# The statements behind the steady loop of a cross-attention kernel, in another order

## The chip, the cores and the metric

The kernel runs on one core of one Trainium2 chip. The metric is the device time of one execution in microseconds (us). The engines are TensorE (PE; its weight loads are PEld), VectorE (DVE), ScalarE (ACT), GpSimd (POOL) and SyncE (SP, which here only issues transfers). Each has its own stream of instructions and waits for the others by semaphores.

## The reference

Cross-attention between a text x (64 batches of 256 x 512) and a context c (64 batches of 256 x 384), all in fp32, with a layer norm on queries, on keys and on the result. For each batch:

```python
text_p  = x @ W_text + b_text            # 256 x 512
audio_p = c @ W_audio + b_audio          # 256 x 512
Q = layer_norm(text_p, g1, beta1)
K = layer_norm(audio_p, g2, beta2)
alpha = softmax(Q @ K.T / sqrt(512))     # 256 x 256
H = (alpha @ audio_p) @ W_out + b_out
out = layer_norm(H + x, g_out, beta_out)
```

## The kernel before

One batch is one step. As the rows of alpha add up to one, alpha @ audio_p @ W_out is taken as (alpha @ c) @ W with one folded weight (`wao_sb`, 384 x 512), and its bias goes in with the start values. The projections and the output product of most batches are done in schemes that save multiplications: the class `Thirds` (L543, keys `k` and the output `o`) multiplies sums of thirds of the operands with sums of thirds of the weights, in steps `one` to `five` (all at L557), between which ScalarE and VectorE put start values into PSUM (`copy_t`, `start_l0`, `start_u`, `take_m`, ...) and evict at the end (`plus_middle`, `plus_ends`, `last_00`, ...). `Fork` (L717) does the same for the queries. `Attention` (L806) holds one batch's scores, softmax, context and output.

The work of a batch is spread over several steps of `for b in range(3, B - 3)`, and `nc` runs under a manual schedule: each engine executes its instructions in the order in which the statements are written. The order is written out, so that a statement of one batch stands between those of three or four others. What hangs together are the data and buffers only: an engine whose next instruction isn't ready waits, and what stands behind it waits with it.

Behind the loop there are some 330 statements that finish the last batches. In them `last_m3` and `old` are batch 60, `settled` and `old_m3` batch 59, `settled_m3` batch 58, `last` and `at_m3` batch 61, `at` batch 62 and `end` batch 63, the last; `q2_m3` and `k2_m3` are batch 63's projections. What the later parts need of them:

- **The round trip of queries and keys.** The normalised rows (`normalise`, ScalarE, L488; in the profile `kr` or `qr`) are stored to memory (`store`, SyncE, L498: `kd<-kr`, `qd<-qr`), fetched back in squares by four transfers (`fetch`, which ends in `squares`, L73: `kq<-kd`, `qq<-qd`) and transposed by VectorE (`turn`, L76). ScalarE then puts gain and bias on (`affine`, L527: `kT`, `qT`), and `score` (L823; by blocks L900) can multiply. SyncE also loads the rows of x and c and stores the results (`out_dram`).
- **The context.** `transpose_e` (TensorE, L978) turns the attention rows `e` into PSUM, `copy_e` (ScalarE, L984) brings them to `eT`, `context_one` and `context_two` (TensorE, L1095) multiply by c, and `copy_one` (L1111) and `copy_two` (L1114) bring the result `zT` out of `ps_z`.
- **The output of batches 62 and 63.** It is done by ordinary products: `multiply` (TensorE, L1192), `multiply_half` (L1236) and `multiply_halves` (L1251), evicted by VectorE (`evict`, L1201; `evict_total`, L1292; `evict_halves`, L1265).
- **The last layer norm.** `totals` (GpSimd, L1140), `deviation` (ScalarE, L1158), `last_deviation` (L422, L424), `shift` (VectorE, L1348), `scale_row` (ScalarE, L1362), `settle` (VectorE, L1357) or `lift_rows` (GpSimd, L1366). For batch 63, row block 0 is finished in a tile `w`: `total_mean` (GpSimd, L1303), `centre_row` (ScalarE, L1307) and `gain_half` for both halves (GpSimd, L1313), then half 0 by `scale_half` (ScalarE, L1323) and `lift_half` (GpSimd, L1327), half 1 by `settle_beside` (VectorE, L1331), and `store_beside` (SyncE, L1334). Row block 1 goes by `evict_halves`, `last_scale` (ScalarE, L422 and L424), `last_shift` (VectorE, L1341) and `settle_half` (VectorE, L1279), and is stored at L1369.

Of the kernel before, what the change touches and what calls it, by code (L numbers as in the profile page):

```python
# [9 lines left out]
F32 = mybir.dt.float32  # L10
# [5 lines left out]
P = 128  # L16
# [6 lines left out]
def kernel(  # L23
# [20 lines left out]
    B, L, D = x.shape  # L44
# [1353 lines left out]
    done = None  # L1398
# [719 lines left out]
    k2_m3 = k[B - 1] = Thirds('k', B - 1, cs.pop(B - 1), wa_blocks, ba_sb, ba_delta)  # L2118
    k2_m3.one()
    last_m3 = att[B - 4]  # L2120
    last_m3.fetch_e()
    k2_m3.copy_n1()
    at_m3.affine_queries(1)
    k2_m3.start_t()
    old_m3.z_part(3)
    old_m3.z_part(4)
    old_m3.z_part(2)
    old_m3.copy_top()
    k2_m3.two()
    at_m3.query_sums()  # L2130
    at_m3.query_step(0)
    k2_m3.three()
    at_m3.affine_queries(2)
    k2_m3.copy_t()
    load_x_rows(B - 4)
    settled_m3 = att.pop(B - 6)
    settled_m3.totals()
    old_m3.add_c21()
    q2_m3.six()
    old_m3.copy_two()  # L2140
    at_m3.affine_queries(3)
    settled_m3.deviation(0)
    done.store()
    k2_m3.start_l1()
    old_m3.start_products(n=0)
    old_m3.zsides.add(1)
    old_m3.zsides.add(1)
    old_m3.zsides.add(1)
    at_m3.take_scores()
    at_m3.score_block(7)  # L2150
    old_m3.zsides.add(1)
    settled_m3.deviation(1)
    k2_m3.start_l0()
    at_m3.keep_p7()
    at_m3.query_step(1)
    settled_m3.last_deviation()
    q2_m3.start_q3()
    q2_m3.step_r()
    at_m3.query_step(2)
    k2_m3.four()  # L2160
    k2_m3.take_m()
    q2_m3.five()
    k2_m3.start_u()
    q[B - 2].turn()
    k2_m3.five()
    q2_m3.after_five()
    k2_m3.copy_n()
    k2_m3.leave_ends()
    k[B - 2].turn([0])
    at_m3.score_block(1)  # L2170
    old_m3.zsides.add(1)
    k[B - 2].turn([1])
    att[B - 2] = Attention(B - 2)
    att[B - 2].affine_queries(2)
    att[B - 2].affine_queries(3)
    old_m3.o.seed()
    q2_m3.two()
    att[B - 2].affine_queries(1)
    old_m3.zsides.add(1)
    at_m3.spread_p1()  # L2180
    old_m3.o.one()
    q2_m3.three()
    att[B - 2].affine_keys(1)
    k2_m3.copy_u()
    k2_m3.middle_d()
    settled_m3.shift(1)
    at_m3.score_block(6)
    att[B - 2].affine_queries(0)
    att[B - 2].affine_keys(2)
    at_m3.keep_v3()  # L2190
    q2_m3.four()
    at_m3.score_block(5)
    at_m3.query_step(3)
    k2_m3.middle_sum()
    k2_m3.leave_middle()
    old_m3.o.copy_n1()
    old_m3.o.two()
    var_m3 = small.tile([P, 4], F32, tag='var4', name='var')
    q2_m3.square(var_m3[:, :2], [0])
    old_m3.o.start_t()  # L2200
    k2_m3.leave()
    old_m3.o.three()
    at_m3.leave_22()
    at_m3.score_block(2)
    att[B - 2].affine_keys(0)
    k2_m3.square(var_m3[:, 2:], [0])
    k2_m3.square(var_m3[:, 2:], [1])
    load_c_rows(B - 3)
    last_m3.turn_e()
    old_m3.zsides.add(1)  # L2210
    at_m3.score_block(3)
    at_m3.score_block(4)
    at_m3.leave_21()
    old_m3.o.copy_t()
    q2_m3.square(var_m3[:, :2], [1])
    last_m3.context_one()
    scales_of(q2_m3, k2_m3, var_m3)
    old_m3.o.start_l0()
    at_m3.maxima()
    at_m3.exponentials([0])  # L2220
    at_m3.exponentials([1])
    q2_m3.normalise([0])
    q2_m3.normalise([1])
    old_m3.o.start_l1()
    old_m3.o.four()
    last_m3.context_two(0)
    old_m3.o.take_m()
    old_m3.o.start_u()
    last_m3.context_two(1)
    old_m3.o.five()  # L2230
    k2_m3.normalise([0])
    last_rows(B - 2)
    q2_m3.store()
    at_m3.reciprocals()
    settled_m3.settle(1)
    last_m3.copy_two()
    last_m3.copy_one()
    settled, old, last = (att[B - 5], att[B - 4], att[B - 3])
    old.start_products(n=0)
    old.zsides.add(1)  # L2240
    old.zsides.add(1)
    old.zsides.add(1)
    att[B - 2].affine_keys(3)
    at = att[B - 2]
    at.score(0, 1)
    at_m3.divide_e([0])
    at.score(1, 2)
    at.score(2, 3)
    at.score(3, 4)
    old_m3.o.plus_middle(x_rows[B - 5], 1)  # L2250
    old_m3.o.plus_ends(x_rows[B - 5])
    k2_m3.normalise([1])
    at.score(4, 5)
    old.o.seed()
    old.zsides.add(1)
    old.o.two()
    old.zsides.add(1)
    old_m3.o.plus_n0()
    at_m3.divide_e([1])
    at.score(5, 6)  # L2260
    old_m3.o.last_11()
    settled_m3.shift(0)
    old_m3.o.last_01(x_rows[B - 5])
    last.transpose_e(bank[4])
    old_m3.o.last_10()
    at.score(6, 7)
    at.score(7, 8)
    old.zsides.add(1)
    old_m3.o.plus_middle(x_rows[B - 5], 0)
    old_m3.o.last_00()  # L2270
    old.o.one()
    last.copy_e()
    at.maxima()
    old.o.copy_n1()
    at.exponentials([0])
    add_bias(B - 2, [0])
    last.context_one()
    settled.totals()
    at.exponentials([1])
    old.o.start_t()  # L2280
    old.o.three()
    settled.deviation(0)
    at.reciprocals()
    settled_m3.settle(0)
    old.o.copy_t()
    old.o.start_l1()
    at.transpose_e(bank[5])
# [189 lines left out]
```

## Time and profile before

| what | value |
|---|---|
| time, median of 3 runs | 1339.95 us (1339.59 to 1342.54) |
| span of the profiled execution | 1339.3 us |
| instructions in it | 29970 |
| busy share: PE, DVE, ACT, POOL | 99%, 93%, 87%, 86% |
| granted TensorE clock from 1277.6 to 1334.2 us | 1.00 |
| TensorE busy from 60 to 1240 us | 1179.54 of 1180.00 us |
| from 1277.6 to 1300, from 1300 to 1327 us | 22.40 of 22.40, 27.00 of 27.00 us |
| last store issued | 1336.01 us |

Of the profiled execution only the span is given; the median of the timed runs is 0.65 us longer. Times in the rows count from the start of the span. A row of a timeline names start, length, engine, line, operation and the tiles (written <- read); the bracket at its end is the idle time before it and what ended it. An instruction's length reaches past the start of the next one where they overlap, so what an engine needs for a row of equal instructions is the distance of their starts.

### The profile page before, as it was taken

What the parts mean: (1) busy time and instruction counts of PE and PEld (TensorE: products, weight loads), DVE (VectorE), ACT (ScalarE), POOL (GpSimd) and SP (SyncE); (2) the same over time, 40 slices, a digit from 0 to 9 for tenths busy, and PEclk for the clock granted to TensorE, in tenths of its full rate; (3) what the DMA queues carried; (4) which work ended last, traced back from release to release, by engine and by line L of the source; (5) the groups of instructions that cost most, each with busy time, mean ns of one, the idle gap of its engine ahead of it and who ended that gap; (6) DMA issues with size and microseconds to landing.
All of it is one profiled execution on the core that took longest, in us unless ns stands there. A gap on an engine that the chain in (4) does not pass through costs nothing.

```text
span 1339.3 us, 29970 instructions
## 1 busy us (share of the span) xinstructions
PE 1329.3 (99%) x8495; PEld 1249.0 (93%) x8495; DVE 1243.7 (93%) x3313; ACT 1163.0 (87%) x3310; POOL 1153.9 (86%) x1855
## 2 busy tenths in 40 slices
PE   8999999999999999999999999999999999999998
PEld 4889999999999999999999999999999999999996
DVE  5769999999999999999999999999999999999968
ACT  4898898988988988988988988989889889889885
POOL 5778898898988988988988988989989889889865
PEclk9999999999999999999999999999999999999999
DMA  8898888889888898889889888899888989888773
GB/s 207 220 247 229 249 244 233 261 242 245 253 251 236 252 253 232 253 230 263 251 242 248 249 239 255 242 238 267 244 235 254 253 236 255 246 237 257 209 225 142
DMA packets 448972, 322.24 MB, mean 241 GB/s; under 512 B 153765, under 2 KB 381349, under 8 KB 448806
## 3 DMA queue, kind: packets, MB, share of 16 engines
q1 hardware_dynamic: 448710, 320.20, 86.0%
q8 instruction: 68, 1.11, 0.4%
q14 instruction: 98, 0.80, 0.2%
q10 hardware_dynamic: 96, 0.13, 0.0%
HBM read 203.57 MB, written 116.65 MB: 239 GB/s over the span
## 4 chain that ended last, share of the span: by engine, by line
PE 97%; ACT 1%; DMA 1%; SPq 0%; issue 0%; DVE 0%; DVEq 0%; ACTq 0%
PE ps_f L733 28%; PE ps_m L557 16%; PE ps_sc L884 13%; PE ps_n L557 11%; PE ps_u L557 8%; PE ps_z L1033 7%; PE ps_l L557 5%; PE ps_z L1095 5%; PE ps_sc L823 1%; DMA eq<-ed 0%; PE ps_f L440 0%; PE ps_n L440 0%; PE ps_l L244 0%; PE ps_m L244 0%; PE ps_u L440 0%; PE ps_fold L244 0%
## 5 line engine op out<-in xcount | busy, mean ns | idle before, releaser
L352 POOL TENSOR_TENSOR csum<-csum,cT 128x256 f32<-128x256 f32 x310 | 195.3, 630 | 5.2
L869 POOL TENSOR_TENSOR qsum<-qT 128x256 f32<-128x256 f32 x118 | 113.1, 959 | 99.0 <-ACT qT L527 92.8
L733 PE MATMUL ps_f<-wtsum,xsum 128*128 128x256 f32 x756 | 194.1, 379 | 0.0
L527 ACT ACTIVATE qT<-qT,columns 128x256 f32<-128x256 f32 x256 | 152.4, 597 | 1.8 <-DVE qT L76 1.8
L733 PEld LDWEIGHTS ps_f<-wtsum,xsum 128*128 128x128 f32 x756 | 131.9, 191 | 11.5 <-issue 0.7
L527 ACT ACTIVATE kT<-kT,columns 128x256 f32<-128x256 f32 x256 | 141.6, 609 | 0.0
L733 PE MATMUL ps_f<-wt,xT 128*128 128x256 f32 x504 | 129.5, 379 | 0.0
L884 PE MATMUL ps_sc<-kT,qT 128*128 128x128 f32 x928 | 122.5, 275 | 0.0
L884 PEld LDWEIGHTS ps_sc<-kT,qT 128*128 128x128 f32 x928 | 114.7, 192 | 0.0
L1357 DVE SCALAR_TENSOR_TENSOR yr<-yr,rstd,beo 128x512 f32<-128x512 f32 x120 | 107.4, 895 | 0.1
L884 PE MATMUL ps_sc<-ksum,qsum 128*128 128x128 f32 x696 | 106.3, 275 | 0.3 <-DVE ps_sc L541 0.2
L884 PEld LDWEIGHTS ps_sc<-ksum,qsum 128*128 128x128 f32 x696 | 97.6, 191 | 4.6 <-DVE ps_sc L541 1.8
L733 PEld LDWEIGHTS ps_f<-wt,xT 128*128 128x128 f32 x504 | 91.0, 190 | 9.7
L1348 DVE SCALAR_TENSOR_TENSOR yr<-yr,nm,go 128x512 f32<-128x512 f32 x124 | 96.4, 778 | 0.0
L488 ACT ACTIVATE kr<-kr,rstd 128x512 f32<-128x512 f32 x126 | 92.5, 736 | 0.1
L314 POOL TENSOR_TENSOR xsum<-xT 128x256 f32<-128x256 f32 x124 | 90.4, 729 | 0.0
L1158 ACT ACTIVATE junk<-yr,nm 128x512 f32<-128x512 f32 x124 | 90.1, 727 | 0.2
L794 ACT ACTIVATE junk<-ps_f 128x512 f32<-128x512 f32 x126 | 75.3, 598 | 16.9 <-PE ps_f L733 15.4
L541 DVE TENSOR_TENSOR ps_l<-ps_m,t 128x171 f32<-128x171 f32 x248 | 83.5, 337 | 6.8 <-ACT t L605 2.3
L804 ACT ACTIVATE qr<-ps_f,rstd 128x512 f32<-128x512 f32 x126 | 87.9, 700 | 0.1
L520 DVE STREAM_TRANSPOSE kT<-kq 128x512 f32<-128x512 f32 x122 | 85.3, 701 | 1.4 <-DMA kq<-kd 1.4
L1095 PE MATMUL ps_z<-eT,c 128*128 128x256 f32 x296 | 84.4, 380 | 0.0
(302 smaller groups left out, 4654.4 us busy)
## 6 DMA issues: line engine op xcount, KB each, us to landing
kd<-kr SPq DMA_DIRECT2D x64, 512.0 KB, 3.1
kq<-kd SPq DMA_DIRECT2D x256, 128.0 KB, 3.3
qd<-qr SPq DMA_DIRECT2D x64, 512.0 KB, 3.0
qq<-qd SPq DMA_DIRECT2D x256, 128.0 KB, 2.8
xq<-in_x_dram SPq DMA_DIRECT2D x252, 128.0 KB, 3.3
x<-in_x_dram SPq DMA_DIRECT2D x63, 512.0 KB, 5.5
out_dram<-yr SPq DMA_DIRECT2D x62, 512.0 KB, 4.6
cq<-in_ctx_dram SPq DMA_DIRECT2D x252, 96.0 KB, 4.3
```

The costliest lines, as they stand in the source:

```text
L314: self.engine.tensor_tensor(*step)
L352: nc.gpsimd.tensor_tensor(*step)
L488: nc.scalar.mul(row, row, self.r[t])
L527: nc.scalar.activation(self.T[:, k, :], self.T[:, k, :], AF.Identity, bias=bet[:, k : k + 1], scale=gam[:, k : k + 1],)
L557: nc.tensor.matmul(place, lhsT=self.sides.of[n], rhs=self.weights[n], start=(n == 14), stop=True, skip_group_check=True,)
L733: nc.tensor.matmul(place, lhsT=side, rhs=w, start=(n == 7 and c == 0), stop=True, skip_group_check=True,)
L869: nc.gpsimd.tensor_tensor(*self.steps[n])
L884: nc.tensor.matmul(self.place(t, m), lhsT=self.qsides[n][:, c], rhs=self.ksides[n][:, c], start=False, stop=True, skip_group_check=True,)
L1033: nc.tensor.matmul(self.zp[{1: 0, 2: 0, 4: 2}.get(n, 1)], lhsT=self.asides[n], rhs=self.bsides[n], start=(n == 7), stop=True, skip_group_c ...
L1095: nc.tensor.matmul(ps, lhsT=c_rows[self.b][:, s, bass.ts(j, P)], rhs=self.eT[:, s, :], start=start, stop=(s == ST - 1), skip_group_check=True,
L1348: nc.vector.scalar_tensor_tensor(row, row, self.nm[:, t : t + 1], go_sb, ALU.add, ALU.mult)
L1357: nc.vector.scalar_tensor_tensor(self.y[:, t, :], self.y[:, t, :], self.r[t], beo_sb, ALU.mult, ALU.add)
```

## The change

The statements behind the loop stand in another order; none is added, taken away or given other arguments. The loop and all ahead of it stay. The start of the rewritten part, and the last third of batch 63's work:

```diff
     q2_m3 = q[B - 1]
-    q2_m3.seven()
+    k2_m3 = k[B - 1] = Thirds('k', B - 1, cs.pop(B - 1), wa_blocks, ba_sb, ba_delta)
+    settled_m3 = att.pop(B - 6)
+    last_m3 = att[B - 4]
     old_m3 = att[B - 5]
     old_m3.context_two(0)
+    old_m3.context_two(1)
+    settled, old, last = (att[B - 5], att[B - 4], att[B - 3])
+    q2_m3.seven()
     at_m3 = att[B - 3]
+    k2_m3.one()
+    k2_m3.two()
+    at_m3.affine_queries(1)
     at_m3.affine_queries(0)
-    old_m3.context_two(1)
+    old_m3.start_products(n=0)
+    k2_m3.copy_n1()
+    old_m3.z_part(3)
+    at_m3.affine_queries(3)
+    old_m3.z_part(4)
+    k2_m3.start_t()
+    old_m3.z_part(2)
+    at_m3.affine_queries(2)
+    old_m3.copy_two()
+    at_m3.query_sums()
+    k2_m3.three()
+    at_m3.take_scores()
+    old_m3.copy_top()
+    last_m3.fetch_e()
+    old_m3.add_c21()
...
     last.o.take_m()
     last.o.start_u()
+    last.o.five()
+    old.shift(0)
+    end.exponentials([0])
+    last.o.plus_middle(x_rows[B - 3], 1)
+    last.o.plus_ends(x_rows[B - 3])
+    last.o.last_01(x_rows[B - 3])
+    at.scales(0, 1)
+    last.o.plus_n0()
+    last.o.last_10()
+    end.exponentials([1])
+    last.o.plus_middle(x_rows[B - 3], 0)
+    end.transpose_e(bank[5])
+    old.scale_row(0)
+    last.o.last_11()
+    old.lift_rows(1, 1)
+    end.copy_e()
+    end.reciprocals()
+    last.o.last_00()
+    last.totals()
+    at.multiply_half(1, bank[4], 0)
     at.shift(0)
-    last.o.five()
-    end.maxima()
-    end.exponentials([0])
-    end.exponentials([1])
-    old.shift(1)
-    last.o.plus_ends(x_rows[B - 3])
-    old.scale_row(1)
-    last.o.plus_middle(x_rows[B - 3], 1)
-    end.reciprocals()
-    at.multiply_half(1, bank[4], 0)
-    end.transpose_e(bank[5])
+    end.context_one()
+    last.deviation(0)
+    end.context_two(0)
+    at.settle(0)
     at.multiply_half(1, bank[4], 1)
-    last.o.plus_n0()
-    at.scales(0, 1)
-    last.o.plus_middle(x_rows[B - 3], 0)
-    last.o.last_00()
-    last.o.last_01(x_rows[B - 3])
-    end.copy_e()
-    end.context_one()
-    old.scale_row(0)
-    old.lift_rows(1, 1)
-    at.settle(0)
+    last.deviation(1)
+    end.context_two(1)
+    last.shift(0)
     old.lift_rows(0, 1)
     end.copy_one()
-    last.o.last_11()
-    end.context_two(0)
-    last.o.last_10()
+    last.last_deviation()
+    old.store()
     at.evict(1)
-    last.totals()
-    last.deviation(0)
+    last.scale_row(0)
+    end.copy_two()
+    at.shift(1)
+    last.lift_rows(0, 1)
+    end.multiply(0, bank[0])
     at.scale_soon(1)
-    at.shift(1)
-    end.context_two(1)
-    end.copy_two()
-    last.deviation(1)
-    last.shift(0)
-    end.start_output()
-    end.multiply(0, bank[0])
-    old.store()
     last.shift(1)
-    last.last_deviation()
-    last.scale_row(0)
-    last.scale_row(1)
-    last.lift_rows(0, 1)
-    at.settle(1)
     end.multiply_halves(1, bank[1:3])
     end.evict_total(0)
-    at.store()
+    at.settle(1)
     end.total_mean(0)
+    end.gain_and_bias([bank[3], bank[5]])
+    end.evict_halves(1, [0])
+    last.scale_row(1)
+    end.evict_halves(1, [1])
     end.centre_row(0)
     last.lift_rows(1, 1)
+    at.store()
     end.gain_half(0, 0)
+    end.gain_half(0, 1)
     end.centred_deviation(0)
-    end.gain_half(0, 1)
-    end.evict_halves(1, [0])
-    end.gain_and_bias([bank[3], bank[5]])
-    end.evict_halves(1, [1])
+    end.scale_half(0, 0)
+    end.lift_half(0, 0)
+    end.last_shift(1)
+    end.settle_beside(0, 1)
+    end.last_scale(1)
+    end.settle_half(1, 1)
+    end.settle_half(1, 0)
     last.store()
-    end.last_scale(1)
-    end.scale_half(0, 0)
-    end.last_shift(1)
-    end.settle_half(1, 0)
-    end.settle_half(1, 1)
+    end.store_beside(0)
     end.store(1, 1)
-    end.lift_half(0, 0)
-    end.settle_beside(0, 1)
-    end.store_beside(0)
```

What that does to an engine's stream is seen in its rows. First ScalarE, at the end of the program. `zT<-ps_z` is batch 63's copy of its context, `junk,ssq<-yr` the two deviations of batch 61, `eT<-ps_f_91` the copy of batch 63's turned attention rows. Before:

```order
L946 ACTIVATE e_17705,den<-ps_sc,nmx 128x256 x2
L1362 ACTIVATE yr_17467<-yr_17467,rstd 128x512
L984 COPY eT_17738<-ps_f_91 128x512
L1362 ACTIVATE yr_17467<-yr_17467,rstd 128x512
L1111 COPY zT<-ps_z_17741 128x512
L1158 ACTIVATE junk,ssq<-yr_17572,nm 128x512
L1114 COPY zT<-ps_z_17752 128x256
L1158 ACTIVATE junk,ssq<-yr_17572,nm 128x512
L422 ACTIVATE log<-ssq,eps 128x2
```

After:

```order
L946 ACTIVATE e_17708,den<-ps_sc,nmx 128x256 x2
L1362 ACTIVATE yr_17458<-yr_17458,rstd 128x512
L984 COPY eT_17734<-ps_f_91 128x512
L1158 ACTIVATE junk,ssq<-yr_17559,nm 128x512 x2
L1111 COPY zT<-ps_z_17748 128x512
L422 ACTIVATE log<-ssq,eps 128x2
L424 ACTIVATE rstd<-log 128x2
L1362 ACTIVATE yr_17559<-yr_17559,rstd 128x512
L1114 COPY zT<-ps_z_17755 128x256
L1362 ACTIVATE yr_17559<-yr_17559,rstd 128x512
```

The copy to `zT` (L1111), which stood ahead of both deviations (L1158), now stands behind both. One of the scalings of batch 60 (L1362) has gone up out of these rows.

The second place is SyncE at the round trip of batch 63's queries and keys. Before:

```order
L498 DMA qd_17459<-qr_17220 128x2x512
L498 DMA kd_17545<-kr_17268 128x2x512
L73 DMA qq_17555<-qd_17459 32x8x128 x4
L73 DMA kq_17560<-kd_17545 32x8x128 x4
L1369 DMA out_dram<-yr_17022 128x2x512
```

After:

```order
L498 DMA qd_17491<-qr_17220 128x2x512
L97 DMA x_17495<-in_x_dram 128x2x512
L73 DMA qq_17526<-qd_17491 32x8x128 x4
L498 DMA kd_17572<-kr_17260 128x2x512
L1369 DMA out_dram<-yr_17022 128x2x512
L73 DMA kq_17584<-kd_17572 32x8x128 x4
```

The store of the keys (`kd<-kr`) now comes after the fetch of the queries (`qq<-qd`), and a store of a result stands between it and the fetch of the keys.

The third place is ScalarE ahead of that store: `kr` are the key rows of batch 63, `e` the attention rows of batch 61, `eT` their turned copy. Before:

```order
L488 ACTIVATE kr_17268<-kr_17268,rstd 128x512
L1114 COPY zT<-ps_z_17443 128x256
L1111 COPY zT<-ps_z_17419 128x512
L527 ACTIVATE kT_17350<-kT_17350,columns 128x256
L960 ACTIVATE e_17431<-e_17431,rden 128x256
L488 ACTIVATE kr_17268<-kr_17268,rstd 128x512
L571 COPY ps_m<-bao 128x2x171
L960 ACTIVATE e_17431<-e_17431,rden 128x256
L984 COPY eT_17510<-ps_f_90 128x512
```

After:

```order
L1111 COPY zT<-ps_z_17422 128x512
L1114 COPY zT<-ps_z_17453 128x256
L527 ACTIVATE kT_17334<-kT_17334,columns 128x256
L960 ACTIVATE e_17440<-e_17440,rden 128x256 x2
L488 ACTIVATE kr_17260<-kr_17260,rstd 128x512
L571 COPY ps_m<-bao 128x2x171
L984 COPY eT_17508<-ps_f_90 128x512
L488 ACTIVATE kr_17260<-kr_17260,rstd 128x512
```

The last scaling of `kr` (L488), which stood ahead of `ps_m<-bao`, now stands behind the copy to `eT`.

The last place is VectorE in the closing rows of batch 63, where `y` is its result and `w` the tile beside it. Before:

```order
L1357 SCALAR_TENSOR_TENSOR y_17634<-y_17634,rone,beo 128x512
L1292 SCALAR_TENSOR_TENSOR y_17775,tot<-ps_m,rden,x_17604 128x512
L1265 SCALAR_TENSOR_TENSOR y_17775<-ps_l,rden,x_17604 128x256
L1273 BN_STATS st_17813<-y_17775 128x6
L1265 SCALAR_TENSOR_TENSOR y_17775<-ps_u,rden,x_17604 128x256
L1273 BN_STATS st_17813<-y_17775 128x6
L1275 BN_AGGR mvy<-st_17813 128x2
L1341 SCALAR_TENSOR_TENSOR y_17775<-y_17775,mvy,ps_n 128x512
L1279 SCALAR_TENSOR_TENSOR y_17775<-y_17775,rstd,ps_f_91 128x256 x2
L1331 SCALAR_TENSOR_TENSOR w<-w,rstd,ps_f_91 128x256
```

After:

```order
L1292 SCALAR_TENSOR_TENSOR y_17627,tot<-ps_m,rden,x_17358 128x512
L1357 SCALAR_TENSOR_TENSOR y_17561<-y_17561,rone,beo 128x512
L1265 SCALAR_TENSOR_TENSOR y_17627<-ps_l,rden,x_17358 128x256
L1273 BN_STATS st_17802<-y_17627 128x6
L1265 SCALAR_TENSOR_TENSOR y_17627<-ps_u,rden,x_17358 128x256
L1273 BN_STATS st_17802<-y_17627 128x6
L1275 BN_AGGR mvy<-st_17802 128x2
L1341 SCALAR_TENSOR_TENSOR y_17627<-y_17627,mvy,ps_n 128x512
L1331 SCALAR_TENSOR_TENSOR w<-w,rstd,ps_f_91 128x256
L1279 SCALAR_TENSOR_TENSOR y_17627<-y_17627,rstd,ps_f_91 128x256 x2
```

`settle_beside` (L1331) now stands ahead of the two halves of L1279, and a settling of batch 62 (L1357) has moved behind L1292.

More of the change, by code (lines that the diff above doesn't have):

```diff
@@ new lines @@
+    old_m3.copy_top()
+    last_m3.fetch_e()
+    old_m3.add_c21()
+    at_m3.query_step(0)
+    old_m3.zsides.add(1)
+    q2_m3.six()
+    k2_m3.copy_t()
+    at_m3.score_block(7)
+    k2_m3.start_l1()
+    k2_m3.start_l0()
+    old_m3.zsides.add(1)
+    last_rows(B - 2)
+    settled_m3.totals()
+    k2_m3.four()
+    q2_m3.after_seven()
+    q[B - 2].turn()
+    k[B - 2].turn([1])
+    at_m3.keep_p7()
+    done.store()
+    q2_m3.start_q3()
+    k2_m3.take_m()
+    at_m3.query_step(1)
+    settled_m3.deviation(0)
@@ L2152 @@
[L2152 to L2165, printed above, removed]
+    last_rows(B - 1)
+    at_m3.score_block(6)
+    settled_m3.shift(0)
+    var_m3 = small.tile([P, 4], F32, tag='var4', name='var')
+    att[B - 2].affine_keys(0)
+    k2_m3.leave_middle()
@@ L2251 @@
-    old_m3.o.plus_ends(x_rows[B - 5])
-    k2_m3.normalise([1])
[L2253 to L2269, printed above, removed]
+    old_m3.o.last_11()
@@ L2270 @@
+    at.score(4, 5)
+    at_m3.divide_e([0])
+    at.score(5, 6)
+    q2_m3.store()
+    at.score(6, 7)
+    old.zsides.add(1)
+    load_x_rows(B - 4)
+    old.zsides.add(1)
+    k2_m3.normalise([0])
+    old.o.seed()
+    last.transpose_e(bank[4])
+    at.score(7, 8)
+    old_m3.o.last_10()
+    old_m3.o.plus_middle(x_rows[B - 5], 0)
+    last.copy_e()
+    k2_m3.normalise([1])
+    old.o.one()
     old_m3.o.last_00()
-    old.o.one()
-    last.copy_e()
     at.maxima()
     old.o.copy_n1()
+    old.o.two()
```

287 lines of the change are left out of this document (130 added, 157 removed).

## The prediction

> **What bounds the kernel now.** I read the page first: the engines' busy shares and the chain that ended last.
>
> ```profile
> span 1339.3 us, 29970 instructions
> PE 1329.3 (99%) x8495; PEld 1249.0 (93%) x8495; DVE 1243.7 (93%) x3313; ACT 1163.0 (87%) x3310; POOL 1153.9 (86%) x1855
> PE 97%; ACT 1%; DMA 1%; SPq 0%; issue 0%; DVE 0%; DVEq 0%; ACTq 0%
> ```
>
> TensorE is busy for 99% of the span and carries 97% of the chain. An order of statements gains only where TensorE now waits, or behind its last product. The windows show where that is (span, TensorE's busy time, then the other engines, granted clock).
>
> ```profile
> 1277.60:1300.00 22.40, 22.40 (x143) 21.30 (x142) 14.23 (x35) 19.88 (x54) 12.79 (x22) 1.00 0.68 215
> 1300.00:1327.00 27.00, 27.00 (x145) 23.50 (x143) 22.97 (x61) 16.48 (x44) 16.37 (x25) 1.00 0.45 143
> 1327.00:1334.20 7.20, 7.17 (x23) 4.10 (x22) 6.16 (x14) 5.88 (x17) 5.09 (x6) 1.00 0.44 166
> 1334.20:1339.30 5.10, 0.00 (x0) 0.00 (x0) 1.59 (x4) 0.44 (x2) 0.72 (x1) 0.79 0.45 169
> ```
>
> The tail starts near 1277.6. From there to 1327 TensorE is busy for 49.40 of 49.40 us at clock 1.00, and to 1334.2 it lacks 0.03. The old order wastes nothing that a new one could win. Behind the last product lie 5.1 us. The chain of waits shows what they hold, and SyncE's timeline the last two stores.
>
> ```profile
> 1327.20 2.65 PE ps_m L1192 x6
> 1331.15 1.31 PE ps_u L1251 x6
> 1334.66 0.87 DVE y L1279 x2
> 1335.56 0.35 SPq L1369 DMA_DIRECT2D out_dram<-y  x1
> 1336.01 0.37 SPq L1334 DMA_DIRECT2D out_dram<-w  x1
> ```
>
> TensorE's last chained product ends at 1332.46 (1331.15 + 1.31), and the last store is issued at 1336.01, 3.55 us later; from there to the end of the span at 1339.3 are 3.3 us of landing and closing, which no order shortens. So all that can be won is a part of 3.55 us, while every wait that the new order puts in front of TensorE is paid in full.
>
> **The change part by part.** It adds and removes no operation, so there is no work to price, only waits. I laid the new rows of each engine on the old durations: an instruction starts when its engine is free and its input done (about 0.2 us from one engine's end to the next one's start), and TensorE's products follow one another at the old paces. Most moves come out with cover left: the scores, the shared small PSUM buffers, the row loads, and all other products of the thirds cost nothing. Five places do not.
>
> *Front of the tail.*
>
> ```profile
> 1278.76 0.60 ACT L527 ACTIVATE qT<-qT,columns 128x256 f32<-128x256 f32 x1
> 1279.26 0.36 ACT L1060 COPY zT<-ps_z 128x256 f32<-128x256 f32 x1
> 1279.52 0.60 ACT L527 ACTIVATE qT<-qT,columns 128x256 f32<-128x256 f32 x1
> 1279.65 0.29 DVE L541 TENSOR_TENSOR zT<-ps_z,u 128x128 f32<-128x128 f32 x1 [0.41 <-ACT zT L1060]
> 1280.76 0.61 PE L900 MATMUL ps_sc<-ksum,qsum 128*128 128x128 f32 x4
> 1282.90 1.24 DVE L76 STREAM_TRANSPOSE qT<-qq 128x1024 f32<-128x1024 f32 x1
> 1285.10 0.88 POOL L352 TENSOR_TENSOR zsum<-zsum,zT 128x128 f32<-128x128 f32 x2
> 1286.28 0.74 PE L557 MATMUL ps_n<-wao,zsum 128*128 128x171 f32 x4
> ```
>
> (a) ScalarE's copy out of ps_z (L1060), on which VectorE's add at L541 and with it the buffer for score_block(7) wait, now follows a second affine (0.50, from 1278.76 to 1279.26) and another copy (0.26, as from 1279.26 to 1279.52): it starts at 1280.02 rather than 1279.26, the add ends at 1280.68, and with 0.2 of handing over the product of 1280.76 starts 0.12 late. (b) VectorE's turn of 1.24 us, which stood right behind the start value of ps_u (L541, `ps_u<-ps_m,m`), now stands ahead of it. It begins at 1281.1, behind the start of ps_l, and with three adds in between the value is done 0.13 late for the last batch's fifth product. (c) GpSimd's two last small adds for zsum stand behind two of the query sums; the output product that starts at 1286.28 comes 0.2 late. (d) At about 1307 ScalarE's copy of the turned attention rows stands behind two deviations; cover that was just enough is short by 0.13. These four come to 0.58 us, each from a cover smaller than the row it is made of, so each could as well be nothing or twice as much.
>
> *The last output product (e), the largest term.* These rows are from ScalarE's and GpSimd's timelines; the two of 1316 are the same pair of deviations in the batch before, one directly behind the other.
>
> ```profile
> 1316.76 0.72 ACT L1158 ACTIVATE junk<-yr,nm 128x512 f32<-128x512 f32 x1
> 1317.67 0.72 ACT L1158 ACTIVATE junk<-yr,nm 128x512 f32<-128x512 f32 x1
> 1326.02 0.50 POOL L1140 TENSOR_SCALAR nm<-totals 128x1 f32<-128x1 f32 x2
> 1326.38 0.59 ACT L1111 COPY zT<-ps_z 128x512 f32<-128x512 f32 x1 [1.82 <-PE ps_z L1095]
> 1326.86 0.72 ACT L1158 ACTIVATE junk<-yr,nm 128x512 f32<-128x512 f32 x1
> 1327.58 0.36 ACT L1114 COPY zT<-ps_z 128x256 f32<-128x256 f32 x1
> ```
>
> In before ScalarE waits 1.82 us for the context at ps_z, copies it the moment it is done, and TensorE takes the copy at 1327.20. In after both deviations (L1158) stand ahead of that copy. They need the totals, done on GpSimd at about 1326.0 as now (VectorE's four evictions of that row lose one settle of 0.75 from their midst, but start later by the 0.58 above). The first deviation then starts near 1326.05 and takes 0.91 (1316.76 to 1317.67), the second 0.72 to the copy behind it (1326.86 to 1327.58): the copy starts at about 1327.65, takes 0.59, and TensorE starts at 1328.4 rather than 1327.20 + 0.58 = 1327.78: 0.62 more. It could be 0.3 if the totals come earlier, 0.9 if later. Together TensorE is 1.2 us late at its last products.
>
> *Behind the last product.* On VectorE the second half of w (L1331) now precedes the two halves of L1279, and w's store precedes y's.
>
> ```profile
> 1332.72 1.42 POOL L1313 TENSOR_TENSOR w<-y,go 128x256 f32<-128x256 f32 x2
> 1333.47 0.21 DVE L1275 BATCH_NORM_AGGREGATE mvy<-st 128x2 f32<-128x12 f32 x1
> 1333.78 0.75 DVE L1341 SCALAR_TENSOR_TENSOR y<-y,mvy,ps_n 128x512 f32<-128x512 f32 x1
> 1334.04 0.20 ACT L424 ACTIVATE rstd<-log 128x1 f32<-128x1 f32 x1
> 1335.45 0.47 DVE L1331 SCALAR_TENSOR_TENSOR w<-w,rstd,ps_f 128x256 f32<-128x256 f32 x1
> ```
>
> In before VectorE is done with L1341 at 1334.53, waits for rstd until 1334.66, does the two halves and then L1331, and w is stored at 1336.01. L1331 needs w's gain (L1313, done at 1334.14) and the rstd of its own row block (long done), not that of y's, so it can start when L1341 ends, 2.07 behind the last product (1334.53 − 1332.46); it takes 0.47 and covers the wait for rstd (2.20 behind), the halves 0.87, and y's store goes out 3.4 behind the last product instead of 3.55. The gain is 0.15. With TensorE 1.2 late, w's gain is done at 1334.8 to 1335.3 and L1331 wants it at 1335.7: near, no wait. Were it one, L1331 would hold up both halves, at most 0.3.
>
> The sum is 0.58 + 0.62 − 0.15 = 1.05. Its own bounds are +0.4 (the four small places at a third, e at 0.4) and +1.8 (the small ones at 0.8, e at 0.9, L1331 short by 0.1). The profiled execution has a span of 1339.3, the median of the timed runs is 1339.95; the sum is made on the first and added to the second: **1341.0 us**. A measurement of this kernel tells apart about 0.2%, 2.7 us, so this counts as within it.
>
> **The rivals.**
>
> *1. The last batch's key round trip comes late (slower).* k is normalised, stored to kd, fetched back as kq and turned.
>
> ```profile
> 1295.31 0.37 SPq L498 DMA_DIRECT2D qd<-qr  x1
> 1298.37 0.37 SPq L498 DMA_DIRECT2D kd<-kr  x1
> 1300.58 1.80 SPq L73 DMA_DIRECT2D qq<-qd  x4
> 1302.48 1.87 SPq L73 DMA_DIRECT2D kq<-kd  x4
> 1297.58 0.71 ACT L488 ACTIVATE kr<-kr,rstd 128x512 f32<-128x512 f32 x1
> 1310.35 1.24 DVE L76 STREAM_TRANSPOSE kT<-kq 128x1024 f32<-128x1024 f32 x1
> kd<-kr SPq DMA_DIRECT2D x64, 512.0 KB, 3.1
> kq<-kd SPq DMA_DIRECT2D x256, 128.0 KB, 3.3
> ```
>
> In after the second normalise (L488) stands behind the copy of the turned attention rows (L984), whose transposes come one score step (0.43) later than before: by the walk it ends at about 1302.6 instead of 1298.3. SyncE now fetches qq first, then stores kd at about 1302.8, then an output, and only then fetches kq. With the median landing of 3.1 the fetch is issued from 1305.9 to 1307.4 and lands 3.3 later, at 1310.7; VectorE reaches the turn at about 1311.6, and nothing is lost. With the 5.27 us that lie in before between the store of qd and its fetch (1295.31 to 1300.58), it lands at 1312.8, and from 1311.7 on each tenth delays the score product and all behind it one for one: 1.1 more. Before had 3 us to spare here, after has none. Decided by the landing of kd: over 4.2 us the end is late. If the fetch of 512 KB in pieces or the store of the output ahead of it takes longer still, 2 more is possible. Total +1.8 to +3.5; 0.28, of which 0.15 lies above +2.7.
>
> *2. The front slips more than walked (slower).* ScalarE is busy for 19.88 of 22.40 us there, and GpSimd's adds (0.73 each) sit on the path of (c) and of the product sums behind it. One more place with a whole affine or add too many gives +0.5 to +0.7 each; two or three of them beside the forecast give +2.2 to +3.2. For it: the walk found four places with under 0.25 us of cover. Against: each was walked row by row. 0.13.
>
> *3. Nothing is lost, or a little won.* The deviations come earlier than walked, and the four small places have more cover than I saw; the end alone changes: −0.3 to +0.4. Faster by 2.7 us would need most of the 3.55 behind the last product. 0.08, of which 0.02 is faster.
>
> *4. The clock drops.* The granted clock is 1.00 wherever TensorE works, and falls only once it has stopped: in the last window above it is 0.79, and of the last 1.1 us it is half.
>
> ```profile
> 1338.20:1339.30 1.10, 0.00 (x0) 0.00 (x0) 0.00 (x0) 0.00 (x0) 0.00 (x0) 0.50 0.00 0
> ```
>
> TensorE has no work behind 1334.2, so a pause of some 4 us costs the clock; one of 0.6, as walked, stands in no row. If the key round trip were late by 4 us, the products behind it would start at half pace: 1.05 + 4 gives +5, and some more. The Trainium skill, "TensorE: Matmul & The Clock Gate", in its Part 1 on the clock gate, says that after an idle window of about 3.4 us the clock is halved, and is back only after as long a busy one; by that rule such a late round trip would cost, as an estimate, up to 1.7 us beside its lateness, and gaps of 0.6 us nothing. The trace agrees as far as its 0.50 at the end goes. 0.03.
>
> That the change doesn't do what it says is out: the rows of ScalarE, SyncE and VectorE stand in the new order.
>
> **How the numbers follow.** The forecast (+0.4 to +1.8, within 0.2%) has 0.48. Rival 1 has 0.28 (0.15 slower, 0.13 within), rival 2 0.13 (0.09 slower, 0.04 within), rival 3 0.08 (0.06 within, 0.02 faster), rival 4 0.03 (slower). Faster 0.02, within 0.71, slower 0.27. The likeliest is +1.05, so 1341.0. The range begins at −0.25, where most of rival 3 lies above, and ends at +3.65, to take in rivals 1 and 2 up to their upper ends: 1339.7 to 1343.6.
>
> **What would show it.** Right: TensorE without gaps of over 0.3 us up to L978 of the last batch, then one wait of about 0.6 at L1192 with the copy at L1111 named, both deviations ahead of it, L1331 ahead of L1279 without a wait, and y's store last, near 1337.1. Wrong at the round trip: the first L823 of the last batch waits for a kT affine, VectorE's turn waits for kq, and kd lands over 4.2 us after its issue. Wrong at the front: waits at L557 or L900 for GpSimd's sums. Wrong altogether: TensorE's busy time in the tail stays whole and the end is at 1339 or less.

## The result, and the profile after

Over 21 runs of each the changed order takes 1342.34 us (median, 1340.88 to 1344.77), the old one 1340.56 (1339.27 to 1342.54): a ratio of 1.0014, 95% interval 1.0008 to 1.002, so about 1.9 us more (1.1 to 2.7). The forecast was 1.05 more, with a range from 1339.7 to 1343.6.

The two profiled executions have the same span, 1339.3 us, and the change is still in them. The last product of the queries ahead of the first moved statement shows it (TensorE's timeline of before, then of after):

```profile
1275.19 1.03 PE L733 MATMUL ps_f<-wt,xT 128*128 128x256 f32 x4
```

```profile
1273.72 1.03 PE L733 MATMUL ps_f<-wt,xT 128*128 128x256 f32 x4
```

The profiled run of after came to the tail 1.47 us earlier, by small differences in the prologue and the loop, where the two programs are the same. From the start of this product, called the marked product below, to the end of the span it is 64.1 us in before and 65.6 in after. This stretch, called the tail, leaves out what varies ahead of it, and is what the experiments are compared by. It is 1.5 us longer.

After by windows (its windows lie 1.5 us later in the program than those of before):

```profile
1277.60:1300.00 22.40, 22.26 (x138) 20.40 (x137) 14.86 (x38) 17.77 (x50) 14.18 (x24) 1.00 0.78 238
1300.00:1327.00 27.00, 26.71 (x142) 23.03 (x142) 22.32 (x55) 19.02 (x49) 14.95 (x21) 1.00 0.35 111
1327.00:1334.20 7.20, 6.98 (x22) 3.93 (x22) 6.89 (x16) 3.88 (x10) 5.12 (x6) 1.00 0.38 143
```

TensorE, which lacked 0.03 us in before, now lacks 0.14 in the first and 0.29 in the second; the 0.22 of the third lie behind its last product, which ends at 1333.98. (It loses more time than these 0.43, as a product counts as busy past the start of the next one; the distances of the starts below show it.) What its weight loads waited for, the rows of "issue" left out:

```profile
PEld ps_m L1192 <- ACT zT L1111: 0.7, 1, 0.7
...
PEld ps_sc L823 <- ACT kT L527: 0.5, 1, 0.5
...
PEld ps_m L557 <- DVE ps_u L541: 0.4, 1, 0.4
PEld ps_m L1192 <- ACT zT L1114: 0.3, 1, 0.3
PEld ps_n L557 <- POOL zsum L352: 0.2, 1, 0.2
```

A load that waits holds up its product only by what is left when the products queued ahead of it are done. The timelines of TensorE and ScalarE have the products:

```profile
1281.78 0.60 PE L557 MATMUL ps_n<-wa_thirds,csum 128*128 128x171 f32 x3
1282.52 0.85 PE L557 MATMUL ps_m<-wa_thirds,cT 128*128 128x171 f32 x4
1284.36 0.61 PE L900 MATMUL ps_sc<-ksum,qsum 128*128 128x128 f32 x4
1284.93 0.97 PE L557 MATMUL ps_n<-wao,zsum 128*128 128x171 f32 x4
1325.95 0.59 PE L1095 MATMUL ps_z<-eT,c 128*128 128x256 f32 x2
1326.83 2.84 PE L1192 MATMUL ps_m<-wao,zT 128*128 128x512 f32 x6 [0.29 <-ACT zT L1111]
1324.59 0.72 ACT L1158 ACTIVATE junk<-yr,nm 128x512 f32<-128x512 f32 x1 [2.61 <-POOL nm L1140]
1325.50 0.72 ACT L1158 ACTIVATE junk<-yr,nm 128x512 f32<-128x512 f32 x1
1326.22 0.56 ACT L1111 COPY zT<-ps_z 128x512 f32<-128x512 f32 x1
```

Against the distances at which the same products follow one another in before, the start at 1282.52 and the product behind it have lost 0.41 us, the one at 1284.93 and its next 0.35, and L1192 0.56, where before lost 0.08. Together that is 1.24 us. Counted in one piece, the last half product of TensorE (L1251, below) starts 57.09 us behind the marked product in after and 55.80 in before, so TensorE is 1.29 us late. The rest is behind it, on VectorE, GpSimd and SyncE:

```profile
1324.75 1.71 POOL L1366 TENSOR_TENSOR yr<-yr,beo 128x512 f32<-128x512 f32 x1
1325.44 1.57 DVE L1348 SCALAR_TENSOR_TENSOR yr<-yr,nm,go 128x512 f32<-128x512 f32 x1
1328.04 1.27 POOL L1366 TENSOR_TENSOR yr<-yr,beo 128x512 f32<-128x512 f32 x1 [1.58 <-ACT yr L1362]
1328.65 1.21 DVE L1352 SCALAR_TENSOR_TENSOR y<-y,mvy,go 128x512 f32<-128x512 f32 x1
1330.81 1.46 PE L1251 MATMUL ps_u<-wao,zT 128*128 128x256 f32 x6
1332.69 0.47 DVE L1265 SCALAR_TENSOR_TENSOR y<-ps_u,rden,x 128x256 f32<-128x256 f32 x1
1334.65 0.48 DVE L1331 SCALAR_TENSOR_TENSOR w<-w,rstd,ps_f 128x256 f32<-128x256 f32 x1
1336.04 0.40 SPq L1369 DMA_DIRECT2D out_dram<-y  x1
```

From the start of the last half product (L1251) to the last store it is 5.23 us; in before it was 5.02, from the start at 1330.99 in this row to 1336.01:

```profile
1330.99 1.46 PE L1251 MATMUL ps_u<-wao,zT 128*128 128x256 f32 x6
1332.49 0.48 DVE L1265 SCALAR_TENSOR_TENSOR y<-ps_u,rden,x 128x256 f32<-128x256 f32 x1 [0.35 <-PE ps_u L1251]
```

VectorE waited 0.35 for that product in before and took it 1.50 behind its start; in after it takes it 1.88 behind, without a wait, since VectorE itself is 0.38 late. Its shift L1348 ran 1.57 us instead of some 0.75, and L1352 1.21, each beside a lift (L1366) of GpSimd. From there to the last store the new order is 0.17 quicker than the old one (3.35 against 3.52), so 0.21 is left. 1.29 and 0.21 make the 1.50 by which the last store is later behind the marked product (62.32 against 60.82).

### The profile page after: what moved, and what is told of

It is laid out like the page before. It is cut to its first block, busy times and chain, and to the rows that moved or that the text cites. A ratio compares the mean times of both kernels' runs of the same rounds, so it can differ in the third digit from the quotient of the medians.

```text
span 1339.3 us, 29963 instructions
## 1 busy us (share of the span) xinstructions
PE 1328.8 (99%) x8495; PEld 1248.7 (93%) x8495; DVE 1244.6 (93%) x3313; ACT 1162.9 (87%) x3310; POOL 1154.1 (86%) x1855
## 4 chain that ended last, share of the span: by engine, by line
PE 95%; ACT 2%; issue 1%; DMA 1%; DVE 1%; POOL 0%; SPq 0%; DVEq 0%; ACTq 0%; POOLq 0%
PE ps_f L733 28%; PE ps_m L557 16%; PE ps_sc L884 13%; PE ps_n L557 10%; PE ps_u L557 8%; PE ps_z L1033 7%; PE ps_l L557 5%; PE ps_z L1095 4%; PE ps_sc L823 1%; DMA eq<-ed 0%; PE ps_f L440 0%; ACT kT L527 0%; ACT kr L488 0%; PE ps_l L244 0%; PE ps_n L440 0%
## 5 line engine op out<-in xcount | busy, mean ns | idle before, releaser
L527 ACT ACTIVATE qT<-qT,columns 128x256 f32<-128x256 f32 x256 | 152.0, 597 | 0.0
L527 ACT ACTIVATE kT<-kT,columns 128x256 f32<-128x256 f32 x256 | 141.6, 609 | 0.7 <-DVE kT L76 0.7
L1357 DVE SCALAR_TENSOR_TENSOR yr<-yr,rstd,beo 128x512 f32<-128x512 f32 x120 | 107.1, 893 | 1.0 <-ACT rstd L424 1.0
L1348 DVE SCALAR_TENSOR_TENSOR yr<-yr,nm,go 128x512 f32<-128x512 f32 x124 | 97.8, 789 | 0.1
L1158 ACT ACTIVATE junk<-yr,nm 128x512 f32<-128x512 f32 x124 | 90.2, 727 | 3.8 <-POOL nm L1140 3.5
L488 ACT ACTIVATE kr<-kr,rstd 128x512 f32<-128x512 f32 x126 | 92.6, 737 | 0.1
```

Source lines behind the costliest of these rows:

```text
L488: nc.scalar.mul(row, row, self.r[t])
L527: nc.scalar.activation(self.T[:, k, :], self.T[:, k, :], AF.Identity, bias=bet[:, k : k + 1], scale=gam[:, k : k + 1],)
L1348: nc.vector.scalar_tensor_tensor(row, row, self.nm[:, t : t + 1], go_sb, ALU.add, ALU.mult)
L1357: nc.vector.scalar_tensor_tensor(self.y[:, t, :], self.y[:, t, :], self.r[t], beo_sb, ALU.mult, ALU.add)
```

## The experiments

The table has the marked product's start, the span and the tail (span less start), all from profiles, and the time, a median where there are several runs. The name's first letter tells from which order a kernel is made (a the changed, b the old, h half of each).

| kernel | product | span | tail | time, us (runs) |
|---|---|---|---|---|
| before | 1275.19 | 1339.3 | 64.1 | 1340.56 (21) |
| after | 1273.72 | 1339.3 | 65.6 | 1342.34 (21) |
| a_copy_first | 1274.00 | 1339.6 | 65.6 | 1341.41 (1) |
| a_lift_early | 1275.05 | 1340.5 | 65.4 | 1342.25 (1) |
| a_turn_back | 1275.50 | 1341.2 | 65.7 | 1342.98 (1) |
| b_copy_last | 1273.93 | 1339.9 | 66.0 | 1341.69 (1) |
| h_front | 1275.78 | 1341.4 | 65.6 | 1343.21 (1) |
| h_end | 1274.20 | 1340.7 | 66.5 | 1342.49 (1) |
| a_front | 1273.68 | 1338.9 | 65.2 | 1340.72 (1) |
| b_swap | 1273.63 | 1337.6 | 64.0 | 1340.52 (11) |
| a_k_late | 1274.15 | 1341.4 | 67.2 | 1343.15 (1) |
| a_k_very_late | 1277.39 | 1348.2 | 70.8 | 1350.01 (1) |
| a_fixed | 1273.64 | 1339.5 | 65.9 | 1342.42 (11) |
| a_fixed2 | 1273.53 | 1339.6 | 66.1 | 1341.93 (11) |

Single times differ by what the tail doesn't explain (the start of the product moves by 4 us), so the tail decides. Each tail is that of one profile, but what makes it up comes back: the first gap of the front is 0.41 or 0.42 in all six kernels that have its order, and VectorE takes the last product 1.87 or 1.88 behind its start in the six kernels whose end is that of after, and 1.49 or 1.50 in the four that have it as in before.

**One statement at the end: a_copy_first.**

```diff
     end.context_one()
+    end.copy_one()
     last.deviation(0)
...
     old.lift_rows(0, 1)
-    end.copy_one()
```

> The changed order with one statement moved: batch 63's copy of its context stands ahead of both deviations of batch 61 again. Measured is the tail: from the start of the product L733 ps_f<-wt,xT of the last batch to the end of the span (64.11 us in before, 65.58 in the changed order). Theory A (the end is VectorE's): the wait of TensorE at L1192 of 0.56 us goes, but L1292, L1265 and all behind them start where VectorE lets them, since its shifts there are held up by GpSimd's lifts; tail 65.5, at most 0.1 won. Theory B (the end is TensorE's): what TensorE gains comes off the end; tail 65.0.

The tail stayed at 65.6, near theory A's 65.5. TensorE's wait for the first copy (L1111) went; half of it came back at the second one, which still stood behind a scaling (its load waits 0.9 for `ACT zT L1114`). TensorE's last half product started 0.25 earlier than in after, and VectorE took it 0.27 later behind its start, so that nothing was won: VectorE had the same lateness of its own (its timeline; the marked product's start is 0.28 later in this run than in after's):

```profile
1326.08 1.20 DVE L1348 SCALAR_TENSOR_TENSOR yr<-yr,nm,go 128x512 f32<-128x512 f32 x1 [0.48 <-ACT junk L1158]
1332.99 0.47 DVE L1265 SCALAR_TENSOR_TENSOR y<-ps_u,rden,x 128x256 f32<-128x256 f32 x1
```

**One of GpSimd's lifts: a_lift_early.**

```diff
+    old.lift_rows(0, 1)
     last.totals()
...
-    old.lift_rows(0, 1)
     end.copy_one()
```

> The changed order with one statement moved: GpSimd's second lift of batch 60 stands ahead of the totals of batch 61, so that it runs beside VectorE's evictions from PSUM and not beside its shift. Theory A: VectorE's shift L1348 takes 0.74 us instead of 1.57, VectorE is ready for L1265 when TensorE is, and the last store is issued about 3.4 us behind the last product instead of 3.77; tail 65.2. Theory B: the shift's length is of no use to the end; tail 65.6.

VectorE's and GpSimd's timelines:

```profile
1326.78 0.75 DVE L1348 SCALAR_TENSOR_TENSOR yr<-yr,nm,go 128x512 f32<-128x512 f32 x1
1329.22 0.75 DVE L1352 SCALAR_TENSOR_TENSOR y<-y,mvy,go 128x512 f32<-128x512 f32 x1
1329.40 1.70 POOL L1366 TENSOR_TENSOR yr<-yr,beo 128x512 f32<-128x512 f32 x1 [3.26 <-ACT yr L1362]
1329.95 1.69 DVE L1348 SCALAR_TENSOR_TENSOR yr<-yr,nm,go 128x512 f32<-128x512 f32 x1
```

The first shift is back at 0.75. But VectorE, now earlier, began L1352 just ahead of the next lift, which took 1.70 instead of 1.27, and the second shift behind it took 1.69. Each engine is the one that is held up, by turns. Of the 0.8 that the first shift won, 0.27 was left at the last store (62.05 behind the marked product, 62.32 in after) and 0.1 in the tail, which lies between theory A's 65.2 and theory B's 65.6.

**The front: a_turn_back and a_front.** The first moves `q[B - 2].turn()` and `k[B - 2].turn([1])` behind `k2_m3.start_u()`; the second moves `k2_m3.middle_d()` behind three of `old_m3.zsides.add(1)` as well.

> The changed order with VectorE's turn of batch 62's queries behind the start value of ps_u again. Theory A: the gap of TensorE at L557 ps_m<-wa_thirds,cT (0.41 us) goes, all behind it in the tail moves up by as much, VectorE's shifts too, since they hang on evictions of products; tail 65.2 (65.1 to 65.4). Rival: a later wait eats it (GpSimd's sums or the key round trip); tail 65.6.

> The changed order with VectorE's turn of batch 62's queries behind the start value of ps_u again, as in a_turn_back, and with GpSimd's difference d (L654, 0.54 us) moved behind the sums that it stands in front of. a_turn_back showed the gap of 0.41 gone and one of 0.82 at ps_n<-wao,zsum in its place. If that gap is GpSimd's queue alone, it falls to 0.3 here and the tail to 65.2; if something else holds those sums, it stays at 0.8 and the tail at 65.7.

In a_turn_back the gap at `ps_m<-wa_thirds,cT` was gone and one of 0.82 stood at the sums, 65.7: the rival held. GpSimd's timeline of this run shows why: the difference d, then the three sums.

```profile
1285.25 0.55 POOL L654 TENSOR_TENSOR d<-n 128x171 f32<-128x171 f32 x1
1285.75 1.81 POOL L352 TENSOR_TENSOR zsum<-zsum,zT 128x128 f32<-128x128 f32 x3
```

With d out of the way 0.42 of the 0.82 was left and the tail was 65.2, as expected: two gaps of the front were one stretch of slack, and removing the first alone gave it to the second.

**The copy in the old order: b_copy_last.** `end.copy_one()`, which stood ahead of `last.o.last_11()`, stands behind `last.deviation(1)`.

> The old order with one statement moved: batch 63's copy of its context stands behind both deviations of batch 61. Both theories: TensorE waits at L1192 for the copy; totals done at 1326.45, two deviations, the copy to about 1328.4, TensorE 1.3 us late. Theory A: VectorE has room there in the old order, so the end is 1.2 to 1.4 us late too; tail 65.4. Theory B gives the same. A rival by which the copy's place costs nothing has 64.1.

TensorE's product waited 1.6 us and the tail grew by 1.9, to 66.0 where both theories had 65.4. In the changed order the copy behind both deviations costs 0.56 at L1192, where a half product (L1236) stands between the two contexts and the totals come earlier. The place of one statement has no price of its own.

**The two halves: h_front and h_end.** h_front has the new order ahead of batch 63's first score product and the old one behind it, h_end the other way round.

> A half of the change: the statements that stand ahead of batch 63's first score product in the changed order keep that order, those behind it stand as in the old one. Tail in before 64.1, in the changed order 65.6. If the losses are separate and pass to the end undiminished, the two gaps at the front (0.41 at ps_m<-wa_thirds,cT and 0.33 at ps_n<-wao,zsum) give 64.85, with no wait at L1192 and the old end. Rival (the end sets itself, by VectorE and GpSimd, whatever the front does): 64.1.

> The other half: old order ahead of batch 63's first score product, changed order behind it. If the losses are separate: no gap at the front, the wait at L1192 (0.56, against 0.08 in before) and VectorE 0.4 late at the second L1265 as in the changed kernel, 0.15 of it given back by L1331's new place; tail 64.8. Rival (the wait at L1192 comes from the front's lateness): 64.1 to 64.3.

Neither held. Each half alone is as long as the whole change, or longer: 1.5 and 2.4 against 1.5. Both have a gap ahead of or between the last batch's scores that after does not have (TensorE's timelines of h_front and of h_end, then VectorE's of h_end):

```profile
1317.23 1.13 PE L823 MATMUL ps_sc<-kT,qT 128*128 128x256 f32 x4 [0.46 <-ACT kT L527]
```

```profile
1317.51 0.53 PE L557 MATMUL ps_u<-wao_thirds,csum 128*128 128x171 f32 x2 [1.39 <-DVE ps_u L541]
...
1310.74 2.45 DVE L1348 SCALAR_TENSOR_TENSOR yr<-yr,nm,go 128x512 f32<-128x512 f32 x2
```

In h_front the late key round trip of the new order (VectorE's turn of kq begins 36.75 behind the marked product, 35.16 in before) meets the old order of the affines, in which the last one (L527, at 1316.58) stands behind a copy that waits 0.99 for a product. That costs 0.73; the front costs 0.78, as good as in after, and the old end is kept, and these make the 1.5. So the front's loss did pass to the end whole, and what the expectation lacked is the new gap. In h_end two shifts take 2.45 us instead of 1.5, the first beside two adds of GpSimd (L1387, 2.50 from 1309.27), and the start value behind them is late: 1.6 of the 2.4. The losses of the halves don't add up to those of the whole.

**The end's new order alone: b_swap.**

```diff
     end.last_shift(1)
+    end.lift_half(0, 0)
+    end.settle_beside(0, 1)
     end.settle_half(1, 0)
     end.settle_half(1, 1)
+    end.store_beside(0)
     end.store(1, 1)
-    end.lift_half(0, 0)
-    end.settle_beside(0, 1)
-    end.store_beside(0)
```

> The old order with one part of the change alone: L1331 ahead of the two halves of L1279, and w stored ahead of y. As the prediction worked it out, VectorE fills its wait for rstd with L1331 and the last store goes out 0.15 us earlier: tail 63.95, time within 0.2% of before. Rival: GpSimd's gain of w, or its read of the same memory, holds L1331 up; tail 64.1 to 64.4.

The last store was issued at 1334.36, 60.73 behind the product, against 60.82 in before: 0.09 won, for 0.15 expected. The time says neither way: ratio 1.0001, 0.9992 to 1.001. This is the shortest tail of all.

**The key round trip: a_k_late and a_k_very_late.** Both move `k2_m3.normalise([1])` down, to behind `settled.deviation(0)` and to behind `at.copy_e()` (there with `k2_m3.store()`).

> The changed order with the second normalise of the last batch's key rows moved behind the first deviation of batch 59. In the changed kernel kd was stored at 1301.41, its fetch began 3.12 us later and the last piece had landed at about 1308.6, 1.9 us ahead of VectorE's turn at 1310.46. Here the store goes out about 3.3 us later, so the turn is 1.4 late and the first score product about 1.2 (it had some 0.15 to spare). If rival 1 of the prediction was right in mechanism and only not reached, the tail becomes 66.8 (65.6 in the changed order) with a wait for a kT affine. If the round trip has other cover, 65.6.

> As in a_k_late, with the normalise and the store moved further, behind the copy of batch 62's turned attention rows. The store goes out about 5.4 us later than in the changed kernel, and TensorE stands still for about 3.4 us ahead of the last batch's first score product. If a pause of that length leaves the clock alone: tail 69.0, granted clock 1.00 behind the pause. If it halves the clock for a time, as the prediction's rival 4 has it: 69.5 to 71, with a granted clock under 1.00 in the windows behind the pause. The Trainium skill, TensorE: Matmul & The Clock Gate, Part 1, has the clock halved after an idle window of about 3.4 us, a window that runs freely: by it a pause of 3.4 us is just about or just not enough.

In a_k_late the load of the first score product waited 1.6 for a kT affine, the product came 1.1 late, and 0.4 more went at a context product, whose turned rows were copied later: 67.2, for 66.8 expected. The mechanism is the one that rival 1 had, with the slack of the round trip used up. In a_k_very_late TensorE stood idle for 3.25 us. Its timeline and windows:

```profile
1320.64 0.70 PE L823 MATMUL ps_sc<-kT,qT 128*128 128x256 f32 x2 [3.25 <-ACT kT L527]
1322.07 3.27 PE L823 MATMUL ps_sc<-kT,qT 128*128 128x256 f32 x8
...
1316.00:1320.00 4.00, 1.39 (x4) 0.32 (x2) 2.27 (x4) 0.99 (x2) 0.00 (x0) 1.00 0.54 180
1320.00:1324.00 4.00, 3.36 (x11) 2.95 (x12) 3.71 (x10) 2.74 (x8) 3.16 (x5) 0.68 0.35 131
1324.00:1328.00 4.00, 4.00 (x21) 3.62 (x21) 1.66 (x5) 1.91 (x7) 1.55 (x3) 0.89 0.03 6
```

The granted clock fell only after the pause had ended: by windows of 0.5 us it is 1.00 up to 1321.0, 0.93 in the next, 0.50 from 1321.5 to 1324.5, 0.66 in the next and 1.00 from 1325.0, so it was halved for about 3.4 us. Eight products that take 1.89 us in after (start 1314.55) took 3.27. The tail grew by 5.2, of which 3.4 is the pause and the rest the half clock. So rival 4 exists, at a pause of 3.25 us. A pause of 1.65 (b_copy_last) left the clock at 1.00, and the changed order was nowhere near either; what lies between them no run shows. The Trainium skill, "TensorE: Matmul & The Clock Gate", Part 1, has about 3.4 us for idle windows and as much for the way back. The time at half clock agrees; the pause that was enough here is a little shorter.

**All places put right: a_fixed and a_fixed2.** a_fixed has the moves of a_front and a_copy_first, `end.copy_two()` ahead of `last.last_deviation()`, the lift of a_lift_early, `last.shift(1)` right behind `last.shift(0)`, and `at.shift(1)` behind `end.evict_total(0)`, with `at.scale_soon(1)` behind `last.lift_rows(0, 1)`. a_fixed2 has `last.lift_rows(1, 1)` behind `end.gain_half(0, 1)` besides.

> The changed order with all the places that the traces named put right: the turn and the difference d at the front as in a_front; batch 63's two copies of its context ahead of what followed the deviations; GpSimd's lifts and VectorE's shifts placed so that none runs beside another (the second lift of batch 60 ahead of the totals, both shifts of batch 61 together, the one of batch 62 behind L1292). If these are all the places, only the gap of 0.42 at ps_n<-wao,zsum stays, there is no wait at L1192, each L1348 and L1352 takes 0.75, and the tail is 64.09 + 0.42 - 0.08 - 0.09 = 64.35; time as before within 0.1%. If a place is left out, 64.7 or more.

> a_fixed with one more statement moved: GpSimd's last lift of batch 61 (L1366) behind both gains of w (L1313). In a_fixed TensorE's last product came only 0.38 us later than in before, but VectorE's settle L1357 stood 1.77 us beside that lift, and VectorE took the last product 1.15 late; tail 65.88. If the two engines shut each other out for these operations, L1357 takes 0.75 here, VectorE is at most 0.35 late at the last product, and the tail is 64.5, up to 65.2 if the later store of batch 61 lands last; time as before within 0.15%. If L1357 is slow for another reason, the tail stays at 65.9.

In a_fixed TensorE lost only the 0.42 at the front, and the tail was 65.9 all the same: a place was left out, VectorE's settle L1357. In a_fixed2 the settle that was slow there runs at its length (GpSimd and VectorE of a_fixed, then VectorE, GpSimd and SyncE of a_fixed2):

```profile
1330.24 1.27 POOL L1366 TENSOR_TENSOR yr<-yr,beo 128x512 f32<-128x512 f32 x1
1330.29 1.77 DVE L1357 SCALAR_TENSOR_TENSOR y<-y,rone,beo 128x512 f32<-128x512 f32 x1
```

```profile
1330.17 0.75 DVE L1357 SCALAR_TENSOR_TENSOR y<-y,rone,beo 128x512 f32<-128x512 f32 x1
1332.37 1.28 POOL L1366 TENSOR_TENSOR yr<-yr,beo 128x512 f32<-128x512 f32 x1
1333.68 0.37 SPq L1369 DMA_DIRECT2D out_dram<-yr  x1
1334.36 0.35 SPq L1334 DMA_DIRECT2D out_dram<-w  x1
1335.08 0.35 SPq L1369 DMA_DIRECT2D out_dram<-y  x1
...
1335.00:1336.00 1.00, 0.00 (x0) 0.00 (x0) 0.05 (x1) 0.00 (x0) 0.00 (x0) 0.76 1.01 369
1336.00:1337.00 1.00, 0.00 (x0) 0.00 (x0) 0.00 (x0) 0.00 (x0) 0.00 (x0) 0.50 1.03 385
SPq L2473 <- DMA out_dram<-y: 3.0, 1, 3.0
```

That settles what held L1357. VectorE, busy with gaps of no more than 0.1 ahead of it, still took the last product 1.98 behind its start, 0.48 later than in before. The last store went out 61.55 us behind the marked product, 1.0 earlier than a_fixed's (1336.21, or 62.6) and only 0.7 later than before's, and still the tail was 66.1, where 64.5 to 65.2 was expected: the lift, moved down, took the 512 KB store of batch 61 with it, to 1333.68, and the transfers' engines were full until 1337 (their share is the second number from the end). SyncE waited 3.0 us for the last landing, where it waited 1.8 in before. The prediction had the landing as a piece that no order shortens; an order can lengthen it. Both kernels are slower than the old order: ratios 1.0013 (1.0004 to 1.0022) and 1.0014 (1.0005 to 1.0023). No version was found that beats it by more than b_swap's 0.09.

## Why the prediction was right, point by point

- **TensorE's lateness, 1.2 forecast, 1.29 in the trace.** (e), the largest term, has 0.48 (0.56 less the 0.08 of before) for 0.62, with both deviations ahead of the copy as described: in before's time, that is 1.47 later, the first deviation starts at 1326.06 and the copy at 1327.69, where 1326.05 and 1327.65 were worked out. The four small ones came to 0.76 for 0.58, but otherwise shared out: (b) 0.41 for 0.13 and (c) 0.35 for 0.2, while (a) and (d) cost nothing (the product of (a) starts at 1279.30, 5.58 behind the marked product, and at 5.57 in before). VectorE's turn in (b) began at 1280.09, which is 1281.56 in before's time, instead of 1281.1. And (b) hides a part of (c), as a_turn_back showed. That the four add up so nearly is partly luck: not one of them came out at its size.
- **The end, −0.15 forecast, +0.21 in the trace: the step that failed.** The order of L1331 and L1279 did what was said: L1331 started without a wait as L1341 ended, and it wins 0.17 in after, and 0.09 alone (b_swap). What was wrong is where that step begins. It counts from TensorE's last product ("2.07 behind the last product") and so took VectorE to be ready for it. VectorE was 0.38 late, because two of its operations took 1.57 and 1.21 us beside GpSimd's lifts. The walk took every duration as fixed.
- **So (e) was the largest gap and not the price.** a_copy_first took half of it away and won nothing. The two late engines, TensorE at L1192 and VectorE at its shifts, ran side by side, and mending one of them left the end to the other.
- **Rival 1** wasn't reached: kd was stored at 1301.41, the fetch began at 1304.53, 3.12 later, near the median landing of 3.1. VectorE reached the turn at 1310.46; by the view of the tile kq its last piece was issued at 1305.9 and landed 2.7 later, at 1308.6, so 1.9 us were to spare. a_k_late shows the rival's mechanism: there the turn waits for kq.

```profile
1301.41 0.38 SPq L498 DMA_DIRECT2D kd<-kr  x1
1304.53 1.80 SPq L73 DMA_DIRECT2D kq<-kd  x4
1310.46 1.24 DVE L76 STREAM_TRANSPOSE kT<-kq 128x1024 f32<-128x1024 f32 x1
```

- **Rival 2** is part of what happened: (a) to (c) came to 0.76 for the 0.45 walked, 0.3 more, and not 1 to 2. **Rival 3** is out: TensorE does wait. **Rival 4** was shown at a pause of 3.25 us; in after the longest was about half a microsecond.

The trace has 1.5 for the 1.05 forecast; the timed runs have 1.9 (1.1 to 2.7), which the trace doesn't contradict and doesn't explain further. The difference is smaller than the 2.7 us that the prediction took to be told apart, and 21 runs of each tell it apart all the same.

## What to carry to other kernels

Where the bounding engine has no gap, another order can win only behind that engine's last instruction (0.09 here); walk it by what each moved statement makes late, and give a sum, not a price for each statement: slack that two places share goes to the second when the first is mended, and a gap on one engine may run beside an equal one on another. Ask of each pair that a new order lets run side by side whether they shut each other out, as VectorE's shifts and GpSimd's lifts do here, and of each store that is moved down whether it now stands ahead of the last one in the transfers' queues. When executions differ by more than the change, compare the stretch behind the last instruction that the two programs have in common.

## What the hardware showed

VectorE's operations with two operands of 128x512 in SBUF (L1348, L1352, L1357) and GpSimd's add of the same kind (L1366) shut each other out: 0.75 us alone, 1.57, 1.20, 1.69, 1.21 and 1.77 when GpSimd had started first; 1.70 for GpSimd's 1.27 when VectorE had. In each of the five VectorE's operation ended 0.54 or 0.55 us behind the end of the lift, however early it had started: it stood until the lift was done. VectorE's evictions of a product, which read one operand from PSUM, show nothing of it beside the same lifts: L1292 took 0.74 in before beside the lift that starts at 1330.05, and L1265 0.47 in after beside the one that starts at 1331.98. The Trainium skill, "SBUF — State Buffer", in the section on who interferes with whom, says so: a VectorE instruction with two SBUF inputs contends with a GpSimd one that reads SBUF, the one that starts second is blocked until the first is done, and one with at most one SBUF input is not touched. The runs agree in each of these cases. The prediction should have weighed it.
